# The last sample's layer 3 written as one list of instructions, in a four-layer attention kernel on one core

## The chip, the cores and the metric

The kernel runs on one core of one Trainium2 chip. The metric is the device time of one execution in microseconds; the median of three runs stands for a kernel. The core's engines are named as in the profile: PE (TensorE, the matrix products), PEld (its weight loads, which run beside the products), DVE (VectorE), ACT (ScalarE), POOL (GpSimd) and SP (SyncE, which here issues most transfers).

## The reference, cut to what matters

Sixteen samples of 256 channels and 32 x 32 positions go through four layers. Layers 0 and 2 are group norm and attention with a residual, layer 1 is a small gate, and layer 3, which the change touches, is this:

```python
q = jnp.einsum('qc,bcn->bqn', Wq, xf) + bq[None, :, None]      # 32 rows
k = jnp.einsum('qc,bcn->bqn', Wk, xf) + bk[None, :, None]      # 32 rows
v = jnp.einsum('vc,bcn->bvn', Wv, xf) + bv[None, :, None]      # 256 rows
energy = jnp.einsum('bqn,bqm->bnm', q, k) * scale
energy = jnp.clip(energy, -10.0, 10.0)
attn = jax.nn.softmax(energy, axis=-1)
out = jnp.einsum('bcm,bnm->bcn', v, attn).reshape(B, C, H, W)
return gamma[0] * out + x
```

All of it is in float32.

## The kernel before, in words

The samples are worked in two streams, even samples in one and odd samples in the other, each written as a generator that yields after a small step. The loop at the end of `fast_path` takes one step of either stream in turn, so that one sample's products can run while the other's results are copied. The second stream starts 30 steps later. So sample 14 ends first, and sample 15, the last, is alone at the end. A scheduler places the instructions of each step; within one engine they keep one order, and waits between engines are semaphores.

Layer 3 of a sample is `clipped_attend`. A sample's 1024 positions are two halves of 512. It does, in this order:

- q and k of one half (`qk`, L1072), copied out of PSUM by ACT (L1084) and DVE (L1088), three copies each for a half.
- The values, by a scheme of seven block products instead of eight (`seven`; its products are recorded at L571). The scheme needs sums of input blocks, s1 to s4, which DVE forms (`combine`, L902 to L905), and sums of value blocks, t1 to t4 (`value_sums`, L557 to L561). ACT copies products out of PSUM (L925), DVE adds others to them (L603).
- For each half of the queries and each half of the keys a set of scores (L1107), then their exponentials on ACT (L1123) and the clip of these on DVE (L1128).
- For each half of the queries the weighted sum of the values (`weighted`), again as seven products: b three times, af twice, c twice, named after the PSUM bank that they use. Sums of blocks of e are formed on DVE (L698, L699, L746, L751); ACT copies (L743, L756, L759, L768) and DVE adds (L725) into `acc`; the row sums come as a 129th column and are inverted (L755, L762); `done` scales by them and adds the residual (L732).
- For all but the last half of sample 15 the result is turned from tokens to channels by DVE (`turn_strips`, L494), the bias is added by ACT (L487, eight instructions for a half), and four transfers of 128 KB leave from SP (`store_tokens`, L463).
- For the last half of sample 15, `store_last` transposes the result on PE (L471), adds the bias on ACT for one half of the channels and on DVE for the other (L477, L479), and sends 256 KB from SP and 256 KB from ACT (L481).

After that a product (`badp`, L1202) counts how many row sums lay in the allowed range; DVE makes a word of it (`bad`, L1205), which every engine loads to decide that the general path need not be run.

PSUM has eight banks of 128 x 512; every product above takes one, and gets it when the last reader of an earlier use is done. The tiles `e` and the raw weights share three buffers.

Of the kernel before, what the change touches and what calls it, by code (L numbers as in the profile page):

```python
# [16 lines left out]
P = 128  # L17
C = 256
# [183 lines left out]
def fast_path(nc, tc, k, bad, x, w_l0, w_l2, w_l3, qk_bias, v_bias, tap_idx, out):  # L202
# [7 lines left out]
    with ExitStack() as ctx:  # L210
# [16 lines left out]
        def bank(nm):  # L227
            return ps_m.tile([P, HALF], FP, tag="m", name=nm)
# [236 lines left out]
        def store_last(y, b, h):  # L465

            of = out[b].rearrange("c (g h n) -> h c g n", g=NG, h=NH)
            for c in range(CC):
                ps = bank(f"last_{c}")
                for t in range(TPH):  # L470
                    nc.tensor.transpose(  # L471
                        ps[:, t * P : (t + 1) * P], y[:, t, c * P : (c + 1) * P], k.ident
                    )
                oc = work.tile([P, NG, TPH, STRIP], FP, tag="oc", name=f"oc_{c}", bufs=3)
                src = ps.rearrange("p (t g j) -> p g t j", t=TPH, g=NG)
                if c:
                    nc.scalar.activation(oc, src, AF.Identity, bias=bcol3[:, c : c + 1])  # L477
                else:
                    nc.vector.tensor_scalar(oc, src, bcol3[:, c : c + 1], None, ALU.add)  # L479
                queue = nc.scalar if c else nc.sync  # L480
                queue.dma_start(  # L481
                    of[h, c * P : (c + 1) * P], oc.rearrange("p g t j -> p g (t j)")
                )

# [6 lines left out]
        def turn_strips(y, ts):  # L491

            part = y[:, :, ts].rearrange("p s t j -> p s (t j)")
            nc.vector.transpose(part, part)  # L494
# [69 lines left out]
        def product(terms, fresh=True, lone=True):  # L564
# [4 lines left out]
            for i, (out, pairs) in enumerate(terms):  # L569
                for m, (left, right) in enumerate(pairs):  # L570
# [10 lines left out]
                    elif m == 0 and not lone:  # L581
# [7 lines left out]
                        )  # L589

# [96 lines left out]
        def weighted(e, vt, tv, y, ri, h, nm, last=None):  # L687
# [39 lines left out]
            def done(i):  # L727
                t = h * TPH + i
                to = y[:, :, t, :]
                if last is not None:  # L730
                    to = last[:, i, :].rearrange("p (s j) -> p s j", j=STRIP)
# [321 lines left out]
        def clipped_attend(xt, y, lane, b):  # L1053

# [4 lines left out]
            steps = values(lane, left, right_of(*folded["l3"]), f"l3_{b}")  # L1063
            qt = TPH // 2
            for h in range(NH):
                ps = bank(f"qk3_{b}_{h}")


                for c in range(CC):
                    for i in reversed(range(2)):  # L1070
# [9 lines left out]
                        )  # L1080
                low, high, full = slice(0, PH), slice(PH, P), slice(0, 2 * P)
# [7 lines left out]

                if h:  # L1090
                    combine(left)
# [7 lines left out]
            ri = small.tile([P, NT], FP, tag="ri", name=f"ri3_{b}")  # L1099
            for h in range(NH):  # L1100
                e = expp.tile([P, NT, HALF], FP, tag="e", name=f"e3_{b}_{h}")
# [417 lines left out]
```

## Time and profile before

| what | us |
|---|---|
| median of three runs | 2700.45 |
| the three runs | 2700.41, 2700.45, 2702.32 |
| span of the profiled execution | 2702.3 |
| time of the execution that has this span, by its number the slowest of the three | 2702.32 |
| sample 15's layer 3 begins on PE | 2643.06 |
| last instruction of PE ends | 2695.68 |
| last transfers are issued | 2696.40 (SP), 2696.44 (ACT) |

All positions are microseconds from the start of the span. A page of the profile gives busy time by engine, the busy share in slices, the transfers, the chain of work that ended last and the costliest groups of instructions. The timeline gives instructions in order of time: start, duration, engine, line, operation, output and inputs, shape, count, and in brackets the idle time before them with the instruction that ended it. PE's durations contain the drain of a product, 0.16 us, under which the next product already runs; the distance from one start to the next is what a product costs in a stream. A span of 2702.3 beside a time of 2702.32 leaves nothing around the span.

### The profile page before, as it was taken

To read this page: it belongs to the slowest core of one execution; us is meant where nothing else is said; L and a number is where in the kernel's file an instruction comes from. 1 tells how busy PE (TensorE), PEld (TensorE's weight loads), DVE (VectorE), ACT (ScalarE), POOL (GpSimd) and SP (SyncE) were. 2 spreads that over 40 slices of the span, in tenths; PEclk is the share of its full clock that TensorE was granted. 3 is DMA by queue.
4 is the path that set the end of the run, shared out by engine and by line. 5 is a ranking of instruction groups with operands and counts; after the bars stand their busy time and mean duration, and the time that the engine had idled before them with its cause. 6 is when DMAs were issued, how large, how long until landed. Compare 5 with 4: busy or idle time off the path is not lost.

```text
span 2702.3 us, 47717 instructions
## 1 busy us (share of the span) xinstructions
PE 2658.2 (98%) x18998; PEld 2366.0 (88%) x18998; DVE 2153.9 (80%) x4242; ACT 1327.9 (49%) x2810; POOL 45.4 (2%) x118
## 2 busy tenths in 40 slices
PE   8999999999999999999999999999999999999997
PEld 6888988888988889889889898988989889898897
DVE  7988886888778887788867888678887788868776
ACT  3454455544455445544455544554454544545443
POOL 1000000000000000000000000000000000000000
PEclk9999999999999999999999999999999999999999
DMA  4021111212111120211201212112111121101111
GB/s 115 1 63 48 56 32 24 63 48 63 25 46 50 42 76 9 55 48 48 63 16 48 63 35 61 32 32 63 48 48 32 32 63 55 40 17 34 52 34 41
DMA packets 134823, 123.07 MB, mean 46 GB/s; under 512 B 10689, under 2 KB 125633, under 8 KB 134593
## 3 DMA queue, kind: packets, MB, share of 16 engines
q1 hardware_dynamic: 132720, 118.63, 15.7%
q8 instruction: 152, 2.49, 0.4%
q10 hardware_dynamic: 1872, 1.31, 0.2%
q14 instruction: 79, 0.64, 0.1%
HBM read 69.58 MB, written 50.33 MB: 44 GB/s over the span
## 4 chain that ended last, share of the span: by engine, by line
PE 81%; DVE 13%; ACT 4%; issue 2%; DMA 1%; POOL 0%; DVEq 0%; SPq 0%; ACTq 0%
PE b_l L571 15%; PE c_l L571 11%; PE af_l L571 11%; PE sb_l L571 10%; PE sc_l L571 8%; PE sf_l L571 4%; PE sa_l L571 3%; PE vb_l L571 3%; PE tb_l L571 3%; PE vc_l L571 2%; PE tc_l L571 2%; PE s L1107 2%; DVE e_l L603 1%; DVE vt L603 1%; PE vf_l L571 1%
## 5 line engine op out<-in xcount | busy, mean ns | idle before, releaser
L672 ACT COPY e_l<-sb_l 128x512 f32<-128x512 f32 x384 | 222.5, 584 | 217.9 <-PE sb_l L571 216.7
L571 PE MATMUL sb_l<-t_l,x 128*128 128x256 f32 x1024 | 262.0, 386 | 0.3
L571 PE MATMUL b_l<-vt,e_l 128*128 128x128 f32 x2048 | 251.8, 275 | 0.0
L571 PEld LDWEIGHTS b_l<-vt,e_l 128*128 128x128 f32 x2048 | 244.2, 192 | 5.4 <-issue 2.3
L571 PEld LDWEIGHTS sb_l<-t_l,x 128*128 128x128 f32 x1024 | 180.5, 191 | 40.1 <-ACT e_l L672 11.2
L682 ACT ACTIVATE e_l<-e_l 128x512 f32<-128x512 f32 x256 | 160.9, 630 | 86.6 <-DVE e_l L603 85.7
L684 ACT ACTIVATE e_l<-e_l 128x1024 f32<-128x1024 f32 x128 | 135.5, 1059 | 118.4 <-DVE e_l L603 118.4
L571 PE MATMUL c_l<-tv,cb_l 128*128 128x129 f32 x1536 | 189.0, 275 | 0.2 <-DVE cb_l L698 0.2
L571 PEld LDWEIGHTS c_l<-tv,cb_l 128*128 128x128 f32 x1536 | 180.3, 191 | 6.9 <-PE qk L1072 3.1
L603 DVE TENSOR_TENSOR e_l<-sc_l,e_l 128x512 f32<-128x512 f32 x128 | 88.0, 687 | 116.6 <-PE sc_l L571 114.9
L925 ACT COPY vt<-vb_l 128x512 f32<-128x512 f32 x144 | 84.5, 587 | 147.2 <-PE vb_l L571 146.1
L487 ACT ACTIVATE xr<-xr,bstrip 128x128 f32<-128x128 f32 (+1 forms) x376 | 134.4, 443 | 44.1 <-DVE xr L494 44.1
L1123 ACT ACTIVATE e<-s 128x512 f32<-128x512 f32 x256 | 131.8, 606 | 22.1 <-PE s L1107 21.4
L756 ACT COPY acc_l<-c_l 128x256 f32<-128x256 f32 x96 | 35.4, 368 | 212.3 <-DVE ri_l L755 151.8
L571 PE MATMUL sc_l<-tc_l,xs_l 128*128 128x256 f32 x512 | 134.0, 384 | 2.3 <-DVE vt L603 2.3
L571 PE MATMUL af_l<-tv,e_l 128*128 128x128 f32 x1024 | 131.6, 278 | 4.3 <-ACT e_l L682 4.3
L571 PE MATMUL sc_l<-t_l,xs_l 128*128 128x256 f32 x512 | 133.0, 382 | 0.8
L571 PE MATMUL sa_l<-t_l,x 128*128 128x256 f32 x512 | 132.4, 381 | 0.0
L571 PE MATMUL sf_l<-tc_l,x 128*128 128x256 f32 x512 | 131.7, 380 | 0.0
L571 PE MATMUL sb_l<-tc_l,xs_l 128*128 128x256 f32 x512 | 131.7, 379 | 0.0
L571 PEld LDWEIGHTS af_l<-tv,e_l 128*128 128x128 f32 x1024 | 121.3, 192 | 10.8 <-ACT e_l L682 7.7
L1128 DVE TENSOR_SCALAR e<-e 128x1024 f32<-128x1024 f32 x128 | 83.0, 687 | 59.0 <-ACT e L1123 59.0
(245 smaller groups left out, 5984.6 us busy)
## 6 DMA issues: line engine op xcount, KB each, us to landing
x<-mid_x SPq DMA_DIRECT2D x64, 512.0 KB, 3.3
xr<-in_x_dram SPq DMA_DIRECT2D x64, 256.0 KB, 4.9
mid_x<-t_z SPq DMA_DIRECT2D x128, 128.0 KB, 2.3
mid_x<-t_l SPq DMA_DIRECT2D x128, 128.0 KB, 2.3
x<-in_x_dram SPq DMA_DIRECT2D x62, 256.0 KB, 4.0
out_dram<-xr SPq DMA_DIRECT2D x124, 128.0 KB, 2.3
raw_l<-in_w_l_dram SPq DMA_DIRECT2D x1, 1024.0 KB, 6.9
raw_l<-in_w_l_dram SPq DMA_DIRECT2D x2, 256.0 KB, 5.5
```

Source lines behind the costliest of these rows:

```text
L487: nc.scalar.activation(y[:, s, ts], y[:, s, ts], AF.Identity, bias=bias[:, s : s + 1])
L571: mm = nc.tensor.matmul(out, left, right, start=fresh and m == 0 and (lone or i == 0), stop=(m == len(pairs) - 1), skip_group_check=True,)
L603: nc.vector.tensor_tensor(dst, src, dst, ALU.add)
L672: nc.scalar.copy(block(i, j), ps.rearrange("p (m n) -> p m n", m=2))
L682: nc.scalar.activation(part, part, AF.Exp)
L684: nc.scalar.activation(e[:, m : m + 2, :], e[:, m : m + 2, :], AF.Exp)
L756: nc.scalar.copy(acc[:, hi, c2], c[:, :, :P])
L925: nc.scalar.copy(block(i, j), ps.rearrange("p (m n) -> p m n", m=TPH))
L1107: nc.tensor.matmul(ss[g][:, j * 2 * P : (j + 1) * 2 * P].rearrange("p (t g j) -> p t g j", t=TPH, g=2), qk[gs, mh, 1 - blk, j * P : (j + 1 ...
L1123: nc.scalar.activation(by_strip[:, :, :, qa], ss[g].rearrange("p (m t n) -> p m t n", m=2, t=TPH), AF.Exp,)
L1128: nc.vector.tensor_scalar(part, part, EXP_MIN, EXP_MAX, ALU.max, ALU.min)
```

## The change

The last sample's layer 3 is no longer stepped in turn with the other stream. `clipped_attend` yields for sample 15 until the other stream has ended (`running`), then emits a list, `ending()`, in one go. `in_traced_order` then ties each instruction of PE, DVE and ACT in it to the one before it on the same engine, so that each engine runs them in the order in which they are written; this adds no semaphore. For the other samples the steps are the same as before, cut into functions.

In the list, the order of the work differs from before:

- The value products are begun before q and k; the sums s1 and s2 stand first on DVE.
- The first set of scores, its exponentials and its clips stand between the value products; the first set of scores of the second half stands between the first and second of the weighted products of the first half, the second set after the fifth.
- Sums for the weighted products go into a spare buffer where they had overwritten blocks of e, and the value sums t1 to t4 are formed between other steps.
- Sample 14's last half (`late`) is turned, biased and stored in the middle of the list, not after sample 14's last step.
- The second half's products are ordered b, af, c, b, b, c, af. The last, af, is added with its scale straight from PSUM after the rest has been scaled, and for half of its columns only.
- The result is transposed in four parts of 128 x 256, the part that needs the last product last. ACT alone adds the bias. Four transfers of 128 KB leave, three from SP and one from ACT, each in runs of 64 numbers (256 B) where there were runs of 128 (512 B).

The number and the sizes of PE's products are the same as before. The diff, cut to its core (its indentation reduced):

```diff
-def store_last(y, b, h):
-    of = out[b].rearrange("c (g h n) -> h c g n", g=NG, h=NH)
-    for c in range(CC):
-        ps = bank(f"last_{c}")
-        for t in range(TPH):
-            nc.tensor.transpose(
-                ps[:, t * P : (t + 1) * P], y[:, t, c * P : (c + 1) * P], k.ident
-            )
-        oc = work.tile([P, NG, TPH, STRIP], FP, tag="oc", name=f"oc_{c}", bufs=3)
-        src = ps.rearrange("p (t g j) -> p g t j", t=TPH, g=NG)
-        if c:
-            nc.scalar.activation(oc, src, AF.Identity, bias=bcol3[:, c : c + 1])
-        else:
-            nc.vector.tensor_scalar(oc, src, bcol3[:, c : c + 1], None, ALU.add)
-        queue = nc.scalar if c else nc.sync
-        queue.dma_start(
-            of[h, c * P : (c + 1) * P], oc.rearrange("p g t j -> p g (t j)")
-        )
+def turned_part(y, part, c):
+    ps = bank(f"last_{part}_{c}")[:, : 2 * P]
+    for t in range(2):
+        nc.tensor.transpose(
+            ps[:, t * P : (t + 1) * P],
+            y[:, 2 * part + t, c * P : (c + 1) * P],
+            k.ident,
+        )
+    return ps
...
+def in_traced_order(start):
+    engines = mybir.EngineType.PE, mybir.EngineType.DVE, mybir.EngineType.Activation
+    before = {}
+    for ins in nc.cur_bb.bb.instructions[start:]:
+        if ins.engine not in engines:
+            continue
+        if ins.engine in before:
+            tc.add_manual_dep(
+                ins,
+                before[ins.engine],
+                mybir.DependencyInfo(
+                    mybir.DependencyClass.NoSync, mybir.DependencyReason.DATA
+                ),
+                reason="the last sample's order",
+            )
+        before[ins.engine] = ins.name
...
+    def qk_products(h):
         ps = bank(f"qk3_{b}_{h}")
...
+    def qk_copies(h, ps):
...
+    def score_products(h, mh):
+        ss = [bank(f"s3_{b}_{h}_{mh}_{g}") for g in range(G4)]
...
+    def exponentials(ss, e, mh, a):
+        m = mh * TPH + 2 * a
+        by_strip = e[:, m : m + 2, :].rearrange("p m (t g n) -> p m t g n", t=TPH, g=2)
...
+    def clip(e, mh, a):
+        m = mh * TPH + 2 * a
+        part = e[:, m : m + 2, :]
+        nc.vector.tensor_scalar(part, part, EXP_MIN, EXP_MAX, ALU.max, ALU.min)
...
+    def ending():
+        sums = right_of(*folded["l3"])
+        tv_tile = tvs[lane]
...
+        es = [exps(0), exps(1)]
+        spare = expp.tile([P, NT, HALF], FP, tag="e", name="spare")
+        hp = HALF // 2
...
+        def banks_of(h):
+            return (
+                bank(f"b_end_{h}")[:, : 2 * P].rearrange("p (i c) -> p i c", i=2),
+                bank(f"af_end_{h}").rearrange("p (w i c) -> p w i c", w=2, i=2),
+                bank(f"c_end_{h}")[:, : 2 * (P + 1)].rearrange("p (i c) -> p i c", i=2),
+            )
...
+        vb_ps, va_ps = bank("vb_end"), bank("va_end")
+        v_go("11", "11", vb_ps, lone=False)
+        v_copy(0, 0, vb_ps)
+        v_go("12", "21", va_ps)
+        nc.vector.tensor_tensor(left("s1"), left("21"), left("22"), ALU.add)
+        subtract(left("s2"), left("s1"), left("11"))
+        pss = [qk_products(h) for h in range(NH)]
+        qk_copies(0, pss[0])
+        subtract(left("s4"), left("12"), left("s2"))
+        subtract(left("s3"), left("11"), left("21"))
+        vc_ps, vf_ps = bank("vc_end"), bank("vf_end")
+        v_go("s1", "t1", vc_ps, lone=False)
+        v_go("22", "-t4", vf_ps)
+        qk_copies(1, pss[1])
+        v_copy(1, 1, vc_ps)
+        v_plus(0, 0, va_ps)
+        s00 = score_products(0, 0)
+        exponentials(s00, es[0], 0, 0)
+        clip(es[0], 0, 0)
+        v_go("s2", "t2", vb_ps, fresh=False)
+        v_copy(0, 1, vb_ps)
+        exponentials(s00, es[0], 0, 1)
+        clip(es[0], 0, 1)
+        v_go("s4", "22", vc_ps, fresh=False)
+        v_plus(0, 1, vc_ps)
+        subtract(t1, v_block(0, 1), v_block(0, 0))
+        v_go("s3", "t3", vb_ps, fresh=False)
+        v_copy(1, 0, vb_ps)
+        v_plus(1, 1, vb_ps)
+        v_plus(1, 0, vf_ps)
+        s01 = score_products(0, 1)
+        exponentials(s01, es[0], 1, 0)
+        clip(es[0], 1, 0)
+        exponentials(s01, es[0], 1, 1)
+        clip(es[0], 1, 1)
+        a = a_of(es[0])
+        acc, keep, plus = acc_of(0)
+        s1 = combp.tile([P, TPH, hp], FP, tag="cb", name="s1_end_0")
+        s2, s3, s4 = spare[:, TPH:, :hp], a(1, 0), a(0, 1)
+        b_ps, af, c_ps = banks_of(0)
+        go(a(0, 0), vb(0, 0), b_ps, lone=False)
+        keep(lo, c1, b_ps)
+        nc.vector.tensor_tensor(s1, a(1, 0), a(1, 1), ALU.add)
+        s10 = score_products(1, 0)
+        for i in range(2):
+            exponentials(s10, es[1], 0, i)
+        subtract(s2, s1, a(0, 0))
+        subtract(t2, v_block(1, 1), t1)
+        go(a(0, 1), vb(1, 0), af[:, 0])
+        subtract(s4, a(0, 1), s2)
+        plus(lo, c1, af[:, 0])
+        go(s1, tv1, c_ps, lone=False)
+        keep(hi, c2, c_ps[:, :, :P])
+        nc.vector.reciprocal(ri[:, 2:4], c_ps[:, :, P])
+        subtract(t3, v_block(1, 1), t3)
+        subtract(s3, a(0, 0), s3)
+        go(s2, t2, b_ps, fresh=False)
+        keep(lo, c2, b_ps)
+        subtract(t4, v_block(1, 0), t2)
+        for i in range(2):
+            clip(es[1], 0, i)
+        go(s4, vb(1, 1, P + 1), c_ps, fresh=False)
+        nc.vector.reciprocal(ri[:, 0:2], c_ps[:, :, P])
+        plus(lo, c2, c_ps[:, :, :P])
+        for i in range(2):
+            scaled(y[:, :, i, :], acc[:, i, :], i, y[:, :, i, :])
+        s11 = score_products(1, 1)
+        for row, _ in late:
+            turn_strips(row, half(1))
+        for i in range(2):
+            exponentials(s11, es[1], 1, i)
+            clip(es[1], 1, i)
+        go(s3, t3, b_ps, fresh=False)
+        keep(hi, c1, b_ps)
+        plus(hi, c2, b_ps)
+        for row, row_b in late:
+            for do in in_pairs(row, half(1), bstrip3):
+                do()
+            store_tokens(row, row_b, 1)
+        go(a(1, 1), t4, af[:, 1])
+        plus(hi, c1, af[:, 1])
+        h = NH - 1
+        a = a_of(es[1])
+        acc1, keep, plus1 = acc_of(1)
+        s1 = combp.tile([P, TPH, hp], FP, tag="cb", name="s1_end_1")
+        s2, s4 = (spare[:, :TPH, i * hp : (i + 1) * hp] for i in range(2))
+        s3 = a(1, 0)
+        last = combp.tile([P, TPH, C], FP, tag="cb", name="last")
+        nc.vector.tensor_tensor(s1, a(1, 0), a(1, 1), ALU.add)
+        for i in range(2, 4):
+            scaled(y[:, :, i, :], acc[:, i, :], i, y[:, :, i, :])
+        b_ps, af, c_ps = banks_of(1)
+        go(a(0, 0), vb(0, 0), b_ps, lone=False)
+        keep(lo, c1, b_ps)
+        subtract(s2, s1, a(0, 0))
+        go(a(1, 1), t4, af[:, 1])
+        subtract(s3, a(0, 0), s3)
+        go(s1, tv1, c_ps, lone=False)
+        keep(hi, c2, c_ps[:, :, :P])
+        nc.vector.reciprocal(ri[:, h * TPH + 2 : h * TPH + 4], c_ps[:, :, P])
+        subtract(s4, a(0, 1), s2)
+        turn_strips(y, half(0))
+        go(s2, t2, b_ps, fresh=False)
+        keep(lo, c2, b_ps)
+        adds = in_pairs(y, half(0), bstrip3)
+        for do in adds[:2]:
+            do()
+        go(s3, t3, b_ps, fresh=False)
+        keep(hi, c1, b_ps)
+        plus1(hi, c2, b_ps)
+        plus1(hi, c1, af[:, 1])
+        def done(i, cs):
+            strips = slice(cs.start // STRIP, cs.stop // STRIP)
+            scaled(
+                last[:, i, cs].rearrange("p (s j) -> p s j", j=STRIP),
+                acc1[:, i, cs],
+                h * TPH + i,
+                y[:, strips, h * TPH + i, :],
+            )
+        for i in range(2, 4):
+            done(i, slice(0, C))
+        for do in adds[2:]:
+            do()
+        store_tokens(y, b, 0)
+        go(s4, vb(1, 1, P + 1), c_ps, fresh=False)
+        nc.vector.reciprocal(ri[:, h * TPH : h * TPH + 2], c_ps[:, :, P])
+        plus1(lo, c2, c_ps[:, :, :P])
+        count(ri, f"l3_{b}")
+        for i in range(2):
+            done(i, c1)
+        for i in range(2):
+            done(i, c2)
+        go(a(0, 1), vb(1, 0), af[:, 0])
+        oc = expp.tile([P, 2, CC, NG, 2, STRIP], FP, tag="e", name="oc_end")
+        turned = []
+        for part, c in ((1, 0), (1, 1), (0, 1)):
+            turned.append((part, c, turned_part(last, part, c)))
+        for i in range(2):
+            to = last[:, i, c1].rearrange("p (s j) -> p s j", j=STRIP)
+            scaled(to, af[:, 0, i], h * TPH + i, to)
+        turned.append((0, 0, turned_part(last, 0, 0)))
+        of = out[b].rearrange("c (g h t j) -> h c g t j", g=NG, h=NH, j=STRIP)
+        for n, (part, c, ps) in enumerate(turned):
+            to = oc[:, part, c]
+            nc.scalar.activation(
+                to,
+                ps.rearrange("p (t g j) -> p g t j", t=2, g=NG),
+                AF.Identity,
+                bias=bcol3[:, c : c + 1],
+            )
+            queue = nc.scalar if n == len(turned) - 1 else nc.sync
+            queue.dma_start(
+                of[h, c * P : (c + 1) * P, :, 2 * part : 2 * part + 2], to
+            )
+    ri = small.tile([P, NT], FP, tag="ri", name=f"ri3_{b}")
+    if b == B - 1:
+        while running:
+            yield
+        start = len(nc.cur_bb.bb.instructions)
+        ending()
+        in_traced_order(start)
+        return
...
-        if b == B - 1 and h == NH - 1:
-            last = combp.tile([P, TPH, C], FP, tag="cb", name="last")
-            yield from weighted(e, vt, tv, y, ri, h, f"l3_{b}", last)
-            store_last(last, b, h)
+        yield from weighted(e, vt, tv, y, ri, h, f"l3_{b}")
+        if b == B - 2 and h:
+            late.append((y, b))
+            yield
             continue
-        yield from weighted(e, vt, tv, y, ri, h, f"l3_{b}")
         turn_strips(y, half(h))
         chores[lane].extend(in_pairs(y, half(h), bstrip3))
         chores[lane].append(functools.partial(store_tokens, y, b, h))
...
+    if first in running:
+        running.remove(first)
```

## The prediction

> **What bounds the kernel now.** I read the page first, then the busy time by stage over the last 150 us, and there the timeline of PE and of what PE waits for.
>
> ```profile
> span 2702.3 us, 47717 instructions
> PE 2658.2 (98%) x18998; PEld 2366.0 (88%) x18998; DVE 2153.9 (80%) x4242; ACT 1327.9 (49%) x2810; POOL 45.4 (2%) x118
> ```
>
> PE is busy 98% of the span: TensorE's stream of products is the kernel, and nothing can be won but where PE is not busy. By stage (span, then PE, PEld, DVE, ACT, POOL busy, granted clock, DMA):
>
> ```profile
> 2630.00:2640.00 10.00, 10.00 (x92) 10.00 (x91) 8.84 (x18) 1.49 (x4) 0.20 (x1) 1.00 0.17 44
> 2650.00:2660.00 10.00, 8.82 (x70) 7.38 (x68) 6.97 (x13) 4.73 (x10) 0.00 (x0) 0.83 0.20 53
> 2690.00:2703.00 13.00, 4.51 (x38) 3.98 (x36) 3.96 (x13) 1.06 (x2) 0.20 (x1) 0.80 0.16 47
> ```
>
> Up to 2643 PE has no gap. From then on only sample 15's layer 3 is left and PE waits for it. The timeline of PE holds seven waits (in brackets: idle before, releaser):
>
> ```profile
> 2649.42 1.53 PE L571 MATMUL vc_l<-vc_l,xs_l 128*128 128x128 f32 x8 [2.28 <-DVE xs_l L902]
> ...
> 2658.01 1.13 PE L1107 MATMUL s<-t_qk 32*128 32x256 f32 x12 [0.33 <-DVE vt L603]
> 2661.02 2.21 PE L571 MATMUL b_l<-vt,e 128*128 128x128 f32 x16 [1.87 <-DVE e L1128]
> ...
> 2677.97 0.71 PE L571 MATMUL b_l<-vt,e 128*128 128x128 f32 x4 [1.64 <-DVE e L1128]
> 2679.33 1.60 PE L571 MATMUL b_l<-vt,e 128*128 128x128 f32 x12 [0.65 <-DVE e L1128]
> 2681.94 2.21 PE L571 MATMUL af_l<-tv,e 128*128 128x128 f32 x16 [1.01 <-DVE e L1128]
> ...
> 2694.85 0.83 PE L471 MATMUL last<-ident,last 128*128 128x128 f32 x4 [1.18 <-DVE last L732]
> ```
>
> Together 8.96 us. The first wait shows why: the sum PE needs (L902) stands on DVE behind sample 14's turn and three copies of qk.
>
> ```profile
> 2645.28 1.25 DVE L494 STREAM_TRANSPOSE xr<-xr 128x1024 f32<-128x1024 f32 x1
> 2646.56 1.49 DVE L1088 TENSOR_SCALAR t_qk<-qk,qb 64x256 f32<-64x256 f32 x3
> 2648.08 0.69 DVE L603 TENSOR_TENSOR vt<-va_l,vt 128x512 f32<-128x512 f32 x1
> 2648.69 0.68 DVE L902 TENSOR_TENSOR xs_l<-x 128x512 f32<-128x512 f32 x1
> ```
>
> That wait has a second price. Microsecond by microsecond the granted clock (third number from the end) is halved from about 2650.06 to 2653.5:
>
> ```profile
> 2650.00:2651.00 1.00, 1.00 (x8) 1.00 (x7) 0.98 (x3) 0.34 (x2) 0.00 (x0) 0.53 0.82 207
> 2653.00:2654.00 1.00, 1.00 (x9) 0.88 (x8) 0.00 (x0) 0.00 (x0) 0.00 (x0) 0.77 0.00 0
> ```
>
> 3.4 us at half speed is 1.7 us of lost work.
>
> **The profiled execution and the runs.** Its span, 2702.3, equals the slowest run, 2702.32; the others took 2700.41 and 2700.45. The 1.9 us between them is about this halved stretch, so I take it that the median runs had none. I sum against 2702.3 and carry the clock as a case of its own.
>
> **The change, part by part.**
>
> *Begin once the other sample is through.* Costs nothing: the rows of each engine, set side by side, are the same in both programs until sample 14's last product on PE (row 4648), until its last sum on DVE (4057), ACT (2248) and SP (476). Sample 15's layer 3 starts at 2643.06 in either.
>
> *PE's work.* The same products. From rows: 7 value products at 0.89 (6.25), 2 qk at 1.0 (2.0), 4 score sets at 1.08 (4.3), 14 weighted products at 1.786 (25.0), 8 transposes and the count's product (1.1): 38.7 us. Check on before: 38.7 + waits 8.96 + 7 drains of 0.165 (1.2) + clock 1.7 + nine switches between kinds of product at 0.1 (0.9; "b_l" takes 1.88 ahead of a score set, else 1.786) = 51.4; measured from 2643.06 to the end of the last transposes, 2695.68: 52.6. Of the 1.2 left, two waits for a second clip (0.16 each) and the last four transposes (0.85 for 0.44) give 0.7; 0.5 stays unexplained and I charge it to the new list too.
>
> *The seven waits in the new list*, walked engine by engine with these rows:
> - First wait (2.28): the turn (1.25) moves behind the first half's sums, and the sums s1, s2 (0.69 each) come first on DVE: s1 is ready at 2645.95, PE asks for it at about 2647. Gone.
> - What is late next: the first score set takes two free banks, the bank of qk's first half and that of its second. The last is free when DVE has copied the second half: copies of the first half from about 2647.45 (they wait for ACT's first copy) 1.5, two sums 1.2, copies 1.5: 2651.6. PE gets there at 2643.06 + 3.8 + 1.8 + 0.3 of switches + 0.4 of scores = 2649.3. **New wait of 2.4 us.** Queued behind it on PE are the other three value products, and behind those ACT's exps and the first clip.
> - 0.33 and 1.87: the second score set and the first weighted product now follow clips that stand between the value steps (done at about 2655.6 for 2656). Gone.
> - 1.64, 0.65, 1.01: the second half's scores go between the first half's products, 13 and 5 us ahead of use; the clips end at 2667.7 and 2671.4, the products that read them start at about 2671.5 and 2673. Gone. In their cover DVE has no gap from 2656 to 2676, with 0.4 to 1.0 us to spare at the sums s1, s2 and s4: a DVE that is later than that is passed on to PE.
> - New, 0.6: in the second half the product of s3 follows that of s2 in the same bank, so PE waits for its own drain (0.165) and ACT's copy (0.37).
> - 1.18: one product is left last, two short DVE rows (0.28 each, estimated from 0.48 for twice the size) and three of four transposed parts run under it. Gone.
>
> Twelve switches: 1.2. Sum 38.7 + 1.2 + 2.4 + 0.6 + 0.5 = 43.4: the last transpose ends at 2686.5 instead of 2695.68, 9.2 us earlier.
>
> *After it.* ACT alone now makes the four parts, 0.37 apart (the copy of 256); the last is done and sent 0.75 after the last transpose; before, 0.76. No gain.
>
> *The transfers.* Before, the last issue came 5.86 us ahead of the end:
>
> ```profile
> 2696.44 0.66 ACTq L481 DMA_DIRECT2D out_dram<-oc  x1
> ```
>
> ```profile
> q10 hardware_dynamic: 528, 0.26, 14.9%
> ...
> out_dram<-oc ACTq DMA_DIRECT2D x1, 256.0 KB, 4.3
> ```
>
> ```profile
> out_dram<-xr SPq DMA_DIRECT2D x12, 128.0 KB, 2.3
> ```
>
> Now 4 x 128 KB leave over 1.1 us, in runs of 256 B instead of 512: 2048 packets for 1024. By bytes the last lands 1.3 us sooner after its issue (2.3 for 128 KB, less what is still queued); but ACT and SP must still load the verdict word after their issues (SP's wait for it was 2.9), so at most 0.7 is won. By packets (14.9% of 16 engines over 6.0 us / 528 = 27 ns each, whatever the length) the data takes 3.5 us instead of 1.75 and lands 0.7 later. The Trainium skill, "DMA: Bandwidth & Descriptors", Specifications, speaks against this part: at least 512 B are needed for line rate, below it the engine reads, modifies and writes. No run here shows a 256-B store. By the packet row the end moves by +0.7, by bytes -0.7, by the rule, if it doubles the packet's time, about +4. I take 0, nearest to the rows. SP's four stores of sample 15's first half (0.45 each) end about 1 us ahead of its first part; sample 14's four go out at 2673 into an idle queue.
>
> Sum: 2686.5 + 0.75 + 5.86 = **2693.1**, 9.2 under the profiled execution, 7.3 (0.27%) under the median.
>
> *The clock.* The row: 2.28 us of wait were followed by a halved clock, 1.87 by none. The Trainium skill, "TensorE: Matmul & The Clock Gate", Part 1, says that the gate judges free-running windows of about 3.4 us; so a wait of the new list's 2.4 us halves the clock or not by where it falls, as 2.28 seems to have done in one run of three. By the row alone (over 2.28: always) the sum is 2694.7, by the rule 2693.1 more often than not.
>
> **The rivals** (what this kernel's measurement can tell from no change is about 0.2%, 5.4 us: 2695.05).
> - A, the list works, clock mostly whole: 2693.1. For it: the sum reproduces before to 0.5 us. Chance 0.52.
> - B, the list works, the 2.4 us wait halves the clock in most runs: PE is short of work nowhere for the next 3.4 us, so all of it shows, +1.6: 2694.7. Chance 0.30.
> - C, a lost microsecond or more in the 256-B runs, or DVE late in its 20 us without a gap (5% is 1 us): 2695 to 2697.5, say 2696. Chance 0.13.
> - D, slower: the 256-B runs. The first issue is at 2686.15; the data starts 1.25 us later, as it did before, and 128 packets per engine follow; with 1.3 to land and 1.56 to close, the end is 2690.3 + 128 packets, and passes 2705.9 (0.2% over the median) once a packet costs over 120 ns, 4.5 times the 27 measured. Against it: transfers of 512-B runs already move 320 GB/s here. Chance 0.03.
> - E, the pinned list changes little, as the new wait and its clock eat the gain: needs 9 us of waits I don't see. The order on PE does follow the list. 2700, chance 0.02.
>
> **How the numbers follow.** Faster by over 0.2%: nearly all of A (0.50), two thirds of B (0.20), a little of C (0.02): 0.72. Within: 0.24. Slower: 0.04. Range: A less 0.7 for the transfers and 0.6 for the residue, 2691.8, and 0.6 of error in walked waits, 2691.2; above through B and half of C: 2696.5.
>
> **What would show it.** Right: PE's timeline without waits for e (L1128's successor); one wait of about 2.4 us in the fourth bank of the first score set, one of 0.6 ahead of the second half's b; last transpose near 2686.5. Wrong: DVE named as releaser before the weighted products; a last issue more than 6 us before the end; PE waiting for a clip.

## The result: 2694.85 us, 6.85 us less, with another clock than foreseen

| | before | after |
|---|---|---|
| median, us (runs) | 2701.70 (6) | 2694.85 (6) |
| lowest and highest | 2700.41, 2703.01 | 2694.17, 2696.04 |
| ratio, after to before | | 0.9971, 95% interval 0.996 to 0.9981 |
| span of the profiled execution | 2702.3 | 2693.2 |
| PE starts on sample 15's layer 3 | 2643.06 | 2639.46 |
| last transposes end | 2695.68 | 2686.34 |
| so layer 3 of sample 15 takes | 52.62 | 46.88 |
| of it with the clock halved | 3.41 | 6.83 |
| from there to the end of the span | 6.6 | 6.9 |

The two medians alone give 0.9975; the ratio on record, from the fast runs, is 0.9971. The profiled execution of after has a time of 2694.99 us and a span of 2693.2. The page of after, first lines:

```profile
span 2693.2 us, 47725 instructions
PE 2654.9 (99%) x18998; PEld 2364.0 (88%) x18998; DVE 2152.2 (80%) x4244; ACT 1328.5 (49%) x2813; POOL 45.3 (2%) x118
```

The product count is the same as before and PE's busy time is 3.3 us less; the rest of the 9.1 us between the spans is idle time. One stage of after (span, then PE, PEld, DVE, ACT and POOL busy, granted clock, DMA):

```profile
2650.00:2660.00 10.00, 10.00 (x75) 8.93 (x76) 5.82 (x9) 5.09 (x11) 0.00 (x0) 0.71 0.01 2
```

PE now has no gap between 2650 and 2660 (8.82 busy before), but a busy PE is not a fast one: its granted clock is 0.71 there. The timeline of PE shows both halves of that:

```profile
2645.20 1.05 PE L1099 MATMUL s<-t_qk 32*128 32x256 f32 x6
2648.42 1.54 PE L1099 MATMUL s<-t_qk 32*128 32x256 f32 x10 [2.17 <-DVE t_qk L1092]
2649.90 2.08 PE L562 MATMUL vb_end<-vc_l,xs_l 128*128 128x128 f32 x8
...
2653.47 1.91 PE L562 MATMUL vb_end<-w,x 128*128 128x128 f32 x8
...
2677.10 1.95 PE L562 MATMUL b_end<-tv,spare 128*128 128x128 f32 x16
2679.51 2.05 PE L562 MATMUL b_end<-vt,e 128*128 128x128 f32 x16 [0.46 <-ACT acc_end L1198]
...
2686.03 0.31 PE L469 MATMUL last<-ident,last 128*128 128x128 f32 x1
```

In place of the seven waits, 8.96 us, there are two others, 2.63 us: PE waits in the fourth bank of the first score set for DVE's copies of qk, and ahead of the second half's second b for ACT to empty the bank. No product waits for a sum of the keys, a clip or `last` any more. But right behind the first wait a row of eight value-product instructions takes 2.08 and then 1.91, where such a row takes 1.06 at a whole clock. DVE shows why the wait is there:

```profile
2645.47 0.69 DVE L1158 TENSOR_TENSOR xs_l<-x,xs_l 128x512 f32<-128x512 f32 x1
2646.09 0.68 DVE L1158 TENSOR_TENSOR x<-x 128x512 f32<-128x512 f32 x1
2646.78 1.49 DVE L1092 TENSOR_SCALAR t_qk<-qk,qb 64x256 f32<-64x256 f32 x3
```

The sums s4 and s3 stand ahead of the copies of the second half of qk, whose bank the score set needs; the products that read them start at 2651.77 and 2653.47.

### The profile page after: what moved, and what is told of

The parts are those of the page before. It is cut to its first block, busy times and chain, and to the rows that moved or that the text cites. A ratio compares the mean times of both kernels' runs of the same rounds, so it can differ in the third digit from the quotient of the medians.

```text
span 2693.2 us, 47725 instructions
## 1 busy us (share of the span) xinstructions
PE 2654.9 (99%) x18998; PEld 2364.0 (88%) x18998; DVE 2152.2 (80%) x4244; ACT 1328.5 (49%) x2813; POOL 45.3 (2%) x118
## 4 chain that ended last, share of the span: by engine, by line
PE 80%; DVE 14%; ACT 3%; issue 2%; DMA 0%; POOL 0%; DVEq 0%; SPq 0%; ACTq 0%
PE b_l L562 15%; PE af_l L562 11%; PE c_l L562 11%; PE sb_l L562 10%; PE sc_l L562 8%; PE sf_l L562 4%; PE sa_l L562 3%; PE vb_l L562 3%; PE tb_l L562 2%; PE s L1099 2%; PE vc_l L562 2%; PE tc_l L562 2%; DVE e_l L612 1%; DVE vt L612 1%; PE qk L1073 1%
```

## The experiments

Times of whole runs scatter by more than these edits are worth: 11 further runs of the changed kernel took 2692.53 to 2698.98, 20 of the kernel before 2699.07 to 2707.28. Most of that lies ahead of the change. In 13 profiles PE reached sample 15's layer 3 at 2639.5 to 2646.8 us. So the edits are judged by layer 3 itself, from PE's first product in it to the end of its last transposes. Two profiles of the changed kernel agree on it to 0.01 us (46.88 and 46.88). Each ratio is to the executions of before that ran beside it; their medians lay between 2701.70 and 2703.68, so a ratio and the medians of two rows need not agree.

The mean granted clock of every execution helps as well. In the 13 profiles the clock is halved outside layer 3 only in a stretch that begins at 50 to 56 us (3.41 or 6.83 us long) and over the last 2.8 to 4.5 us. A window of 3.41 us at half clock takes 0.0006 off the mean, so a mean of 0.997 or less leaves at least one halved stretch for layer 3, 0.999 leaves none, and 0.998 does not tell.

| run | layer 3, us | of it at half clock | its end to the span's end | median of the runs (n) | ratio to before, 95% |
|---|---|---|---|---|---|
| before | 52.62 | 3.41 | 6.6 | 2701.70 (6) | |
| before_again | 55.4 | 13.65 | 6.5 | 2702.01 (20) | 0.9994 (0.9987 to 1.0001) |
| after | 46.88 | 6.83 | 6.9 | 2694.85 (6) | 0.9971 (0.996 to 0.9981) |
| after_again | 46.88 | 6.83 | 6.4 | 2694.81 (11) | 0.997 (0.9961 to 0.9979) |
| e1_copies_first | 42.51 | 0 | 6.8 | 2693.13 (6) | 0.9968 (0.9956 to 0.998) |
| e2_product_first | 41.60 | 0 | 6.8 | 2693.14 (5) | 0.9963 (0.995 to 0.9977) |
| e4_warm | 43.83 | 0 | 6.6 | 2692.22 (6) | 0.9967 (0.9955 to 0.9979) |
| e10_warm4 | 43.83 | 0 | 6.2 | 2695.08 (7) | 0.9969 (0.9958 to 0.998) |
| e3_long_runs | 45.33 | 3.41 | 7.0 | 2695.59 (12) | 0.9975 (0.9966 to 0.9983) |
| e5_turn_at_once | 48.95 | 6.83 | 6.6 | 2698.48 (14) | 0.9989 (0.9981 to 0.9997) |
| e6_unpinned | 48.17 | 3.41 | 6.7 | 2697.55 (22) | 0.998 (0.9974 to 0.9987) |
| e8_all | 42.25 | 0 | 6.9 | 2693.74 (5) | 0.9966 (0.9953 to 0.9979) |
| e9_keep_first | 40.73 | 0 | 7.0 | 2691.69 (5) | 0.9956 (0.9942 to 0.9969) |

### The changed kernel again

> The changed kernel once more, unaltered, as the measure for the runs beside it and to see what one execution differs from the next. Theory clock (the 2.17 us wait ahead of the first score set on TensorE sets off the halved stretch that follows it): the stretch stands again between about 2649 and 2656, 6.8 us long, in this profile too, and layer 3 of sample 15 takes 46.9 us to the end of its last transposes. Rival (the halved stretch comes with free-running windows, whatever the wait): it stands elsewhere or is 3.4 us long or is absent, and layer 3 takes 43.5 to 45.2. The common part ahead of it differs by up to 3.5 us from the profile before in either case.

The stretch is there again, 6.83 us from 2650.48 on, 0.38 us after the end of the same wait of 2.17, and layer 3 takes 46.88. The rival's shorter or absent stretch did not come. Of all 17 executions of the changed kernel ten have a mean clock of 0.997, seven 0.998 and none 0.999.

### The wait made shorter, in two steps

```diff
 qk_copies(0, pss[0])
-subtract(left("s4"), left("12"), left("s2"))
-subtract(left("s3"), left("11"), left("21"))
 ...
 qk_copies(1, pss[1])
+subtract(left("s4"), left("12"), left("s2"))
+subtract(left("s3"), left("11"), left("21"))
```

> VectorE copies the second half of qk out of its bank ahead of the sums s4 and s3 of the keys and not behind them. The two sums are 2 x 0.6 = 1.2 us, so the wait of 2.17 ahead of the first score set should fall to about 0.9 to 1.0. Theory clock: with 0.9 us the clock stays whole, so 1.3 + 3.4 = 4.7 us are won against the changed kernel, 2690.2. Rival (the halved stretch has nothing to do with this wait): 1.3 us are won, 2693.6. Rival (the sums are needed as soon as the copies): the time moves to a wait ahead of the value product of s4, 2694.9.

The second step, on top of the first:

```diff
+v_go("s2", "t2", vb_ps, fresh=False)
+v_copy(0, 1, vb_ps)
 s00 = score_products(0, 0)
 ...
-v_go("s2", "t2", vb_ps, fresh=False)
-v_copy(0, 1, vb_ps)
```

> As the run before it, and TensorE takes the value product of s2 (1 us with its switch) ahead of the first score set, with its copy on VectorE. The wait should fall to 0 to 0.4 us. Theory clock: 2.0 + 3.4 us won, 2689.5. Rival (halved stretch of another cause): 2.0 us won, 2692.9. If VectorE's copy of the product comes late, the wait reappears ahead of the next product into that bank.

PE's timeline, first of e1 and then of e2:

```profile
2649.44 1.10 PE L1099 MATMUL s<-t_qk 32*128 32x256 f32 x10 [0.86 <-DVE t_qk L1092]
```

```profile
2650.57 1.10 PE L1099 MATMUL s<-t_qk 32*128 32x256 f32 x10 [0.31 <-DVE t_qk L1092]
```

The waits are 0.86 and 0.31, the score products take 1.10 and not 1.54, and no part of layer 3 runs at half clock. It falls by 4.37 (expected 4.7) and by 5.28 (5.4): the wait and the clock (3.05, next section) together, and in e2 0.37 more that is not traced. The medians fell by 1.7 only. In the profile of e1, PE came to layer 3 2.3 us later than in that of after, 1.7 of it from a halved stretch at 52 us that was 6.83 us long and not 3.41. That is not the edit's doing, and it is why the whole times alone would have misled.

### The wait filled and not shortened

```diff
-s00 = score_products(0, 0)
+s00 = score_products(0, 0, 10)
 # in it, ahead of the scores, ten times:
+nc.tensor.matmul(ss[0][:, :P], left("11")[:, 0], xt[:, 0, 0], start=True, stop=True)
```

> Ten extra products of 128x128 by 128 columns, read by nothing and overwritten, go into the first score bank ahead of the first score set: about 10 x 0.11 = 1.1 us of work for TensorE in a wait of 2.17 us that nobody else needs it in. The wait for VectorE's copies ends at the same time as before, so without the clock nothing changes. Theory clock: TensorE idles only about 1 us, the clock stays whole, and 3.4 us are won, 2691.5. Rival (halved stretch of another cause): 0 won, 2694.9. If the extra products go out behind the wait and not in it, 1.1 us are lost.

> Four extra products, read by nothing, ahead of the first score set in place of ten: they fill 8 rows x 0.12 = 0.96 us of the 2.17, so TensorE idles about 1.2 us in one piece. Theory share (what counts is the idle part of a window of 3.41 us, half or more of it halves the clock): 1.2 is a third, the clock stays whole, layer 3 takes 43.8. Rival (any idle piece of over about 1 us does it): a stretch of 3.4 or 6.8 us follows, 45.3 or 46.9.

The ten products are twenty instructions and take 2.40 us, not the 1.1 expected; they fill the wait:

```profile
2645.31 2.40 PE L1097 MATMUL s<-x 128*128 128x128 f32 x20
2647.63 0.71 PE L1103 MATMUL s<-t_qk 32*128 32x256 f32 x6
2648.62 1.10 PE L1103 MATMUL s<-t_qk 32*128 32x256 f32 x10 [0.28 <-DVE t_qk L1092]
```

The four are eight instructions and leave 1.62 us of idling, more than the 1.2 expected:

```profile
2651.62 1.10 PE L1103 MATMUL s<-t_qk 32*128 32x256 f32 x10 [1.62 <-DVE t_qk L1092]
```

In both profiles the clock stays whole and layer 3 takes 43.83 us, 3.05 less than in the changed kernel, though PE does more and useful work starts no sooner: the ten score instructions behind the wait start 8.96 us into the layer in all three. So the wait of 2.17 halves the clock, and 43.83 is what the list takes with its waits as they are and the clock whole. The rival of another cause is out. The one of e10 ("any idle piece of over about 1 us") is out in that profile: 1.62 in one piece did nothing. But the profile is not the rule for e10: five of its seven executions have a mean clock of 0.997, so by the reckoning above the clock was halved in layer 3 there, and its median, 2695.08, is about that of the changed kernel. Ten filling products kept it whole in at least four of six executions (0.999; the other two 0.998), four in two of seven.

### Long runs in two transfers

```diff
-oc = expp.tile([P, 2, CC, NG, 2, STRIP], FP, tag="e", name="oc_end")
+oc = expp.tile([P, CC, NG, TPH, STRIP], FP, tag="e", name="oc_end")
 ...
+if n < 2:
+    continue
 queue = nc.scalar if n == len(turned) - 1 else nc.sync
-queue.dma_start(of[h, c * P : (c + 1) * P, :, 2 * part : 2 * part + 2], to)
+queue.dma_start(of[h, c * P : (c + 1) * P], oc[:, c].rearrange("p g t j -> p g (t j)"))
```

> The result leaves in two transfers of 256 KB with runs of 512 B (one 128-channel half each, after its second part) in place of four of 128 KB with runs of 256 B. Everything ahead of the transfers stays. Theory short runs (256-B runs cost the tail): from the last transpose to the end of the span falls from 6.4 to 6.9 us to 5.7 to 6.0, and the time by 0.7 to 1. Rival (the tail is the closing of the program, whatever the transfers): it stays within 0.3. Rival (four smaller transfers do help): it grows by up to 0.7, as the last transfer is 256 KB and not 128.

The end stays where it was, 7.0 us behind the transposes (6.2 to 7.0 with four transfers). The queues' packets over the end, first of the changed kernel (2686 to 2693.2), then of e3 (2685 to 2693); the share is of 16 engines:

```profile
q1 hardware_dynamic: 1752, 0.47, 28.4%
q10 hardware_dynamic: 528, 0.13, 8.8%
```

```profile
q1 hardware_dynamic: 782, 0.38, 17.1%
q10 hardware_dynamic: 528, 0.26, 12.6%
```

As means, that is (28.4% + 8.8%) x 16 x 7.2 / 2280 = 19 ns for a packet with runs of 256 B, and (17.1% + 12.6%) x 16 x 8 / 1310 = 29 ns with 512 B. Shorter runs cost engine time (2048 packets x 19 / 16 = 2.4 us for the result against 1024 x 29 / 16 = 1.9), and neither way moves the end. The edit changes the length of the runs and the number of transfers at once: the first of four parts leaves before the last is ready, and a gain from longer runs may be offset by the later start of the two. The two were not separated. Layer 3 took 1.55 us less in this run because the same 2.17 us wait was followed by one halved window and not two; nothing ahead of the transfers was edited.

### The late turn undone, the pin undone

```diff
-for row, _ in late:
-    turn_strips(row, half(1))
 ...
-for row, row_b in late:
-    for do in in_pairs(row, half(1), bstrip3):
-        do()
-    store_tokens(row, row_b, 1)
 ...
-if b == B - 2 and h:
-    late.append((y, b))
-    yield
-    continue
```

> Sample 14's last half is turned, biased and stored at once, as before the change, and not behind the first half of sample 15. VectorE's turn (1.25 us) then stands ahead of the four sums of the keys, and ScalarE's eight bias rows (2.5) ahead of its last copy of qk's first half. Theory order (the late turn is what let the sums come in time): a wait of 1 to 1.5 us ahead of the first product that reads a sum is back, and the wait ahead of the first score set falls on top to 3.4 to 4.7 us less that; layer 3 of sample 15 grows from 46.9 by 1.3 to 2.5 us, more if a third window at half clock follows (1.7). Rival (the turn is hidden anyway): 46.9 as now.

PE's timeline of e5:

```profile
2645.43 1.16 PE L562 MATMUL vc_end<-vc_l,xs_l 128*128 128x128 f32 x8 [0.35 <-DVE xs_l L1221]
...
2648.74 0.70 PE L1099 MATMUL s<-t_qk 32*128 32x256 f32 x4 [1.25 <-DVE t_qk L1092]
2649.85 0.67 PE L1099 MATMUL s<-t_qk 32*128 32x256 f32 x2 [0.41 <-DVE t_qk L1092]
2652.68 2.04 PE L1099 MATMUL s<-t_qk 32*128 32x256 f32 x10 [2.17 <-DVE t_qk L1092]
```

and a row of ACT and one of DVE:

```profile
2645.22 2.45 ACT L478 ACTIVATE xr<-xr,bstrip 128x128 f32<-128x128 f32 x8
2648.19 1.51 DVE L1092 TENSOR_SCALAR t_qk<-qk,qb 64x256 f32<-64x256 f32 x3 [2.09 <-ACT t_qk L1088]
```

Layer 3 grows by 2.07 us, as much as the three new waits, 0.35 + 1.25 + 0.41 = 2.01. Only 0.35 of it is the sums; the larger part comes through ACT, whose eight bias rows (2.45 us) stand ahead of its last copies of qk, and DVE's copies wait for those. The expected size was right, its place was not: what the late turn frees first is ACT.

```diff
-in_traced_order(start)
```

> The same list of instructions of sample 15's layer 3, but not pinned: the scheduler orders each engine by its own costs. TensorE's order stays but for three products; VectorE puts a copy of values (0.69) and sample 14's turn (1.25) ahead of the sums, and ScalarE the eight bias rows ahead of qk's second half. Theory order: the waits of before come back ahead of the first product that reads a sum (about 1.9 us) and ahead of the score set, layer 3 takes 48 to 51 us (before 52.6, changed kernel 46.9). Rival (the gain lies in TensorE's order of products alone): 46.9, or 46.4 since the three products stand in its second wait of 0.46.

Layer 3 takes 48.17 us with one halved window, and PE waits again where it did before (PE's timeline of e6):

```profile
2652.52 1.16 PE L562 MATMUL vc_end<-vc_l,xs_l 128*128 128x128 f32 x8 [1.92 <-DVE xs_l L1221]
...
2659.94 1.16 PE L562 MATMUL vb_end<-w,x 128*128 128x128 f32 x8 [0.71 <-ACT vt L1149]
...
2672.51 2.05 PE L562 MATMUL c_end<-vt,e 128*128 128x129 f32 x16 [0.64 <-DVE ri L1271]
```

PE's order is the same but for three products, which went ahead of the second half's s3, so PE's order alone is not the gain; the rival (46.9 or 46.4) is out. Against the list with one halved stretch of 3.41 us, 45.33 (e3), the pin is worth 2.8 us.

### The second wait, missed and then hit

Both edits stand on top of e2. Not shown in the excerpts: the order of one sum and of the transposed parts changed with them.

```diff
+go(s4, vb(1, 1, P + 1), c_ps, fresh=False)    # with its reciprocal, plus1, count and done
 go(s3, t3, b_ps, fresh=False)
 keep(hi, c1, b_ps)
 plus1(hi, c2, b_ps)
 plus1(hi, c1, af[:, 1])
-go(s4, vb(1, 1, P + 1), c_ps, fresh=False)
 go(a(0, 1), vb(1, 0), af[:, 0])
```

> The run with the product of s2 ahead of the first score set, and in the second half the product order s2, s4, s3, so that another product stands between the two that share a bank, with the transposed parts in a new order. The 0.46 us wait should go as well: layer 3 of sample 15 falls from 41.6 (that run) to about 41.1 with the clock whole. Rival (the reciprocal, now behind one more sum on VectorE, or the later parts come late): a wait of 0.3 to 0.6 ahead of the transposes takes its place, 41.6 again.

The 0.46 went, but a longer wait came one product later, and layer 3 takes 42.25, more than the 41.60 of e2 and more than either expectation (PE of e8):

```profile
2681.75 2.05 PE L562 MATMUL af_end<-vt,e 128*128 128x128 f32 x16 [1.25 <-DVE acc_end L1201]
```

The last product writes the other half of af's bank. It must wait until DVE has added the half that is there, and that addition now stood behind the copy of s3's product, which had moved back. The cure turns the order of the two round:

```diff
 go(a(1, 1), t4, af[:, 1])
+keep(hi, c1, af[:, 1])
 ...
-keep(hi, c1, b_ps)
+plus1(hi, c1, b_ps)
 plus1(hi, c2, b_ps)
-plus1(hi, c1, af[:, 1])
```

> The run with all edits, with the 1.25 us wait ahead of the last product mended: ScalarE copies af's second half (the product of a11 and t4) out at once, and VectorE adds the product of s3 to it afterwards, where before the copy was of s3's product, and af was read only after it. Theory: VectorE then reads af no more after the product of s3, the wait of 1.25 goes and nothing comes for it; layer 3 takes 42.25 - 1.25 = 41.0. Rival (VectorE's six rows after the product of s3 come late for the transposes): a wait of up to 0.5 there, 41.5, as without the edit.

PE of e9 has no wait in this stretch, the transposes follow the last product in its stream, and layer 3 takes 40.73 (expected 41.0):

```profile
2682.13 1.95 PE L562 MATMUL b_end<-vt,e 128*128 128x128 f32 x16
2683.91 1.95 PE L562 MATMUL af_end<-vt,e 128*128 128x128 f32 x16
2685.70 0.94 PE L469 MATMUL last<-ident,last 128*128 128x128 f32 x7
```

This kernel has the lowest median: 0.9956 of the time before (0.9942 to 0.9969), against 0.9971 (0.996 to 0.9981) for the change. Its median is 3.2 us below that of the change; layer 3 is 6.15 shorter. The whole times leave open how much of the 6.15 a median of more runs would show, since the common part ahead differs by up to 7 us from run to run.

### The kernel before again

> The kernel before once more, unaltered. The prediction took it that the median run of before has no halved stretch after its first wait of 2.28 us. Theory clock as the runs now have it (every wait of about 2 us in a piece is followed by one or two windows of 3.41 us at half clock): the stretch is there again, 3.4 or 6.8 us long, and layer 3 of sample 15 takes 52.6 us (54.3 with two windows). What the prediction held: no stretch, 50.9. In either case the layer starts at another time than 2643.06, by up to some us, as the runs of the changed kernel do.

More than expected: three halved stretches, 13.65 us. The waits on PE are those of before, and in this execution the clock answers to three of them (PE of before_again):

```profile
2647.79 1.43 PE L571 MATMUL vc_l<-vc_l,xs_l 128*128 128x128 f32 x8 [2.28 <-DVE xs_l L902]
...
2659.38 3.78 PE L571 MATMUL b_l<-vt,e 128*128 128x128 f32 x16 [1.87 <-DVE e L1128]
...
2679.12 1.12 PE L571 MATMUL b_l<-vt,e 128*128 128x128 f32 x4 [1.65 <-DVE e L1128]
```

The same b_l group after the same 1.87 takes 3.78 here and 2.21 in the first profile. Which windows of 3.41 us the waits fall in tells the two apart. Taking the edges from the halved stretches of each trace, the window of the 1.87, first in the first profile of before, then here (PE busy is the second number):

```profile
2656.89:2660.30 3.41, 1.93 (x28) 1.08 (x20) 3.38 (x7) 3.28 (x8) 0.00 (x0) 1.00 0.01 2
```

```profile
2655.37:2658.78 3.41, 1.81 (x28) 0.96 (x20) 3.38 (x7) 3.28 (x8) 0.00 (x0) 1.00 0.01 2
2658.78:2665.60 6.82, 6.22 (x29) 6.22 (x30) 6.03 (x7) 1.35 (x3) 0.00 (x0) 0.50 0.00 0
```

In the first, the window holds 1.48 us of idling and the clock stays; in the second it holds 1.60, and the clock is halved for the next 6.82. In either case that is the wait of 0.33 and a piece of the 1.87: an edge cuts it into 1.15 and 0.72 in the first and into 1.27 and 0.60 in the second. The same two windows in e3, whose wait of 2.17 is cut into 0.70 and 1.48, and the one ahead of the scores in e10:

```profile
2647.71:2651.12 3.41, 1.93 (x18) 1.60 (x19) 2.00 (x4) 1.08 (x2) 0.00 (x0) 1.00 0.00 0
2651.13:2654.54 3.41, 3.41 (x19) 3.41 (x17) 2.06 (x4) 1.57 (x3) 0.00 (x0) 0.50 0.03 5
```

```profile
2647.84:2651.25 3.41, 2.16 (x20) 1.64 (x18) 3.32 (x7) 1.28 (x3) 0.00 (x0) 1.00 0.00 0
```

Over all 13 profiles, in layer 3: windows that held 1.60, 1.65, 1.92, 2.05, 2.17 (twice) and 2.28 (twice) us of idling were followed by a halved one, windows with up to 1.25 were not, and of two with 1.48 one was (e3) and one was not (before). So what counts in these profiles is how much of a 3.41 us window is idle, with the border near 1.5 us. The windows don't move with the program: from the start of the first halved stretch to that of the one in layer 3 it is 2597.5 us in before and in after alike, 761 windows, though layer 3 begins 2590.6 us behind the first of these edges in before and 2588.1 in after. By that the 1.62 of e10 passed because an edge cut it into 1.25 and 0.37, and was not spared in the five executions with a mean clock of 0.997.

Open: why the 2.17 is followed by two halved windows in three profiles that have it and by one in e3, though in two of the three PE is busy all through the first of them.

## Why the prediction was right or wrong

The forecast, 2693.1, lies 1.75 us from the median, inside the range, and its sign was right. It put the gain at 7.3 us under the median of the three runs; against the median of all six it is 6.85. Term by term it is less good than that, and that the number is so near is partly luck: for the profiled execution the halved clock (+3.05) and the time outside the span (+1.8) were missed, and an earlier start of layer 3 (-3.60), which nothing ties to the change, took most of both back. For the profiled execution (the waits in the list by e4 and e10):

| term | predicted | measured |
|---|---|---|
| layer 3 begins | 2643.06 | 2639.46 |
| list with its waits, clock whole | 43.4 | 43.83 |
| halved clock | 0 (A), 1.6 (B) | 3.05 (46.88 - 43.83) |
| last transpose to last issue | 0.75 | 0.71 |
| last issue to end of span | 5.86 | 6.15 |
| span | 2693.1 | 2693.2 |
| outside the span | 0 | 1.8 |

**"The seven waits in the new list": right.** All seven went. The new wait stands where it was put, for the reason given, with 2.17 us for 2.4, and the second with 0.46 for 0.6. With "PE's work" and its switches the list was sized to 0.4 us; the waits came out 0.4 shorter and the rest 0.8 longer (41.2 for 40.4), which was not traced further. The cover was right too: no row of DVE between 2656 and 2676 makes PE wait. Undoing the late turn (e5) and the pin (e6) brings waits back, so the list's gain is in the order on DVE and ACT as much as on PE.

**"The clock": wrong, and the likeliest case with it.** A held that the 2.4 us wait leaves the clock whole more often than not; both profiles of the changed kernel, and e3, have it halved, and the mean clock says the same of at least ten of its 17 executions. B was the mechanism. Its size, 1.6, is that of one window (e3: 45.33 - 43.83 = 1.50); two windows cost 3.05. The step that failed is the reading of a single profile: "2.28 us of wait were followed by a halved clock, 1.87 by none", and with it "in one run of three": of 106 further executions of before 94 have a mean clock of 0.997 or less and ten 0.999, so a halved clock in layer 3 was the rule there. The Trainium skill, "TensorE: Matmul & The Clock Gate", Part 1, says that the windows are free-running, and the profiles agree with their numbers: the edges keep their distance of 3.41 us while the layer moves, and the 1.87, which falls on them a little otherwise in the second profile of before, is followed by 6.83 halved microseconds. I had the rule and took it to favour A; but by the border of 1.5 us a wait of 2.17 is spared only if an edge leaves less than that on both sides, which holds for 0.83 of the 3.41 us in which the edge can fall, an estimated one execution in four (cut as in e3, 0.70 and 1.48, it was not spared).

**"The profiled execution and the runs": wrong.** The span of 2702.3 was taken for the whole time of the run of 2702.32. Every profile since has a time 1.8 to 1.9 us above its span (2694.99 and 2693.2, 2705.18 and 2703.3), so the profiled execution of before took about 2704.1 and is none of the three runs; and the 1.9 us between those runs say nothing of the clock. The sum of 2693.1 was a span; as a time it would have been 2694.9.

**"Begin once the other sample is through", cost 0: right for the edit, not for the execution.** PE came there 3.60 us earlier than in the profile of before. Two profiles of one kernel differ there by 1.6 or 1.7 us (before 2643.06 and 2641.43; after 2639.46 and 2641.14), and the eleven profiles with the new list, whose code ahead of it is the same, spread over 7.3 (2639.46 to 2646.77), so nothing ties the 3.60 to the change. The 9.1 us between the two spans match the 9.2 predicted, but they are 5.74 from layer 3 and 3.60 from ahead of it, less 0.24 at the end, and not 9.2 from layer 3. The match is chance. What the change brings is better read from the clock-free layer: 43.83 against 52.62 less 1.7 for its one halved window (the prediction's figure), about 7 us; and before loses more to the clock than the changed kernel in some executions (13.65 us halved in one).

**"The transfers", taken as 0: about right.** Last issue to end is 6.15 for 5.86. The 256 B packet took 19 ns: neither as much as the packet row had it (27 ns whatever the length) nor half; and the doubling that I drew from the Trainium skill's 512 B rule ("DMA: Bandwidth & Descriptors", Specifications), +4 us, is not there. The last issue in the timeline of ACT, and the rows of the transfers (KB each, median us from issue to landing):

```profile
2687.05 0.64 ACTq L1372 DMA_DIRECT2D out_dram<-oc_end  x1
```

```profile
out_dram<-oc_end SPq DMA_DIRECT2D x3, 128.0 KB, 2.3
out_dram<-oc_end ACTq DMA_DIRECT2D x1, 128.0 KB, 4.4
```

The fourth transfer lands 4.4 us after its issue although it is half as large as the one of before (4.3). That it is held up by the other three, which are on the same 16 engines, fits but is not shown.

D falls with the result. Of C, the late DVE falls with the timeline of PE; a loss of a microsecond in the short runs would have had to show against e3, and the end did not move, unless the later start of e3's two transfers hid it. E falls with the waits that are gone. B stands.

## What to carry to other kernels

When waits on PE are shortened, add up the idle time that is left per clock window and not per wait: here 2.17 us of idling cost another 3.05 in halved clock, and ten unread products put into the wait, which shorten nothing, gave that back. Decide between edits of a few microseconds by the piece of the trace that they touch: here two profiles agreed on it to 0.01 us while whole times of one kernel scattered by 6 to 8. And when two products share a PSUM bank, look for every reader of that bank before moving one of them: mending a wait of 0.46 made one of 1.25 until the order of its readers was turned as well.

## What the runs showed of the hardware that was not expected

The same wait of 1.87 us is followed by no halved clock in one execution and by 6.83 us of it in another, though its place against the edges differs by 0.12 us only; the granted clock changes at edges 3.41 us apart, with a border near 1.5 us of idling in a window.

A store in runs of 256 B took 19 ns a packet, one in runs of 512 B 29 ns, as means over the last 7 to 8 us: half the bytes cost about two thirds of the time.

The first 60 us of the kernel differ from execution to execution by up to 7 us, more than the change is worth. The first values of the first sample, in the profile of after and in that of e9 (timeline of PE), before any edit of either matters:

```profile
29.58 1.06 PE L562 MATMUL vb_l<-wvp_l,x 128*128 128x128 f32 x8
```

```profile
34.66 1.06 PE L562 MATMUL vb_l<-wvp_l,x 128*128 128x128 f32 x8
```

5.08 us of the 6.74 by which e9 comes later to layer 3 are there already; a halved stretch at 52 to 63 us, 6.83 us in e9 and 3.41 in after, gives the other 1.7. What makes the start late stays open.
